# Near score tiles kept from the maxima pass and turned into the scores, in a fused two-layer kernel

## The chip, the cores and the metric

The kernel runs on one core of one Trainium2 chip, as one launch. The metric is device time in microseconds, taken as the median of several runs. A profiled execution of the same kernel gives the trace and the page that the text quotes. Engines are named as the page names them: PE is TensorE's matrix products, PEld its weight loads, DVE is VectorE, ACT is ScalarE, POOL is GpSimd and SP is the engine that issues most DMAs.

## The reference

Two layers run on x of 2 batches, 1024 tokens and 128 features. Each layer normalises x, and adds an attention and a feed-forward block that both read the normalised x.

- Layer 0: a causal attention with sigmoid in place of softmax, and a mixture of 32 experts (4 of them count for a token) with a shared expert. The kernel computes all experts for all tokens here and weighs them.
- Layer 1: a softmax attention of 16 heads of 8 features, without a causal mask, and a mixture of 16 experts with a shared one. The kernel sorts the tokens by expert, so that each token meets only its 4 experts.

The change lies in layer 1's attention, and in a few steps of the routing beside it. Cut to what matters:

```python
xn = _layernorm(x)
q, k, v = heads(xn @ Wq.T), heads(xn @ Wk.T), heads(xn @ Wv.T)      # 16 heads of 8
att_rel_pos = einsum('bhsd,pd->bhsp', q, pos_emb_k)                  # 256 positions
att_idxs = clip(ar[None, :] - ar[:, None], -128, 127) % 256
att_pos = att_rel_pos[:, :, ar[:, None], att_idxs]
att = softmax((einsum('bhqd,bhkd->bhqk', q, k) + att_pos) / sqrt(8))
y = einsum('bhqk,bhkd->bhqd', att, v)
x = x + merged(y) @ Wproj.T + experts(xn)
```

The position term depends on the distance of key and query, clipped to -128 and 127. For a query tile of 128 tokens it varies with the key only in the key tile of the same number and its two neighbours. These are the "near" tiles. In all key tiles further off it is one number per query on each side, and it can be folded into the keys.

## The kernel before, in words

**Groups and steps.** The 16 heads are handled four at a time: a slot `s` (0 to 3) holds one head in each of four row groups `r` of 32 partitions, and a product uses 32 rows of PE for each head. A group `n` is a batch, a slot and a block `q` of 512 queries (`groups`, L767). There are 16 groups, eight for each batch. Each group takes eight steps, one for each key tile `kt`, so 128 steps in all (loop at L1189). After step 67 (`EXPERTS`, L1157) the experts run in one piece, and the second batch's attention follows.

**Work of one step.** A step `t` does the following on PE, in this order:

- `scores` (L944) for step t. The scores are made turned, keys on partitions and queries along the row. First, for each near query tile, the position tile `near` is transposed into PSUM (L953, against `ident`), for row group 0, then 1, 2, 3. Then a product of keys and `qa` is added over the whole 512 columns (L963). `qa` holds the queries and, in a spare row, the negative maximum of each query. `kls` and `khs` hold the keys with the position constants of the low and the high side, and the product is split in two where the side changes. ScalarE takes the exponential of the four banks into `p` (L970).
- `values` (L974) for step t-1: `p` times `vs` into the accumulator `acc` (L982). In some steps it is split in two halves around the next item (`halved`, L1202).
- `scan` (L891) for a group ten steps ahead (`LEAD`, L768). It makes the scores unturned, for one query tile and one half of the keys (L902), and VectorE takes their maxima: far parts by a plain reduction (L927), near parts together with the `near` tile by a custom operation (L922), which writes the sum to `junk` and the maximum to `maxima`. With the second half of a query tile the two are joined and negated into `negmax` (L930). `augment` (L932) turns `negmax` and adds it to the queries to make `qa` (L937, L941).

**The near tiles.** Twice in a group `positions` (L880) runs. `by_position` (L844) multiplies queries and the position table (L853), ScalarE copies the result to `rel` (L857), and VectorE repeats its last column over 128 more (L859). A DMA takes `rel` to memory (`bounce`, L866), and another brings it back skewed by one element per row as `near` (L877).

**PSUM.** In this stage seven banks go round under the name `sm` (L1142) and one holds `acc`. `scores` and `scan` take four banks each, so a step uses one bank more than there are.

**Beside the steps.** In the first batch the second batch's gate and a counting sort (`gate1`, `sort1`, L507 and L535) run on VectorE, cut into parts by `yield`, and named one or two parts to a step (L1174). The tokens are then scattered to their experts' slots on POOL's queue (L618). In the second batch POOL gathers the experts' results, 64 tiles of 128x128 (`gather`, L626, DMA at L630), from step 68 on, some four in three steps. Each gather may start only after the last exponential of its step (`paced`, L609). Three steps later in the program (L1181) `gathered` (L636) multiplies it by its weight (L640) and adds it to `x2s` (L641), both on POOL. `operands` (L827), also on POOL, makes `kls` and `khs` (L834) and `vs` (L837) for a new slot.

**What sets the order.** The order on PE is that of the program, written out by hand (`manual_schedule`, L1187). On the other engines a planner sets each queue's order before the run, from the times at which it expects an instruction's inputs. Every engine then takes its own queue in order.

## Time and profile before

| what | us |
|---|---|
| median of 3 runs | 1305.56 |
| lowest, highest run | 1305.07, 1309.41 |
| the profiled execution's own time | 1308.08 |
| its span, first to last instruction | 1306.3 |
| exponentials, L970 (512), busy | 264.7 |
| plain maxima, L927 (472 in this stage), busy | 226.7 |
| maxima of near parts, L922 (292 in this stage), busy | 130.3 |
| product of the scores, L963 (832 with `kls`, 512 with `khs`), busy | 112.9 and 60.3 |
| transposes of near tiles, L953 (704), busy | 108.4 |
| multiply and add of gathered tiles on POOL, L640 and L641 (64 each), busy | 41.1 and 30.3 |

Busy time is the union of a group's instructions. Several matmuls run at the same time on different rows of PE, so a group's mean duration times its count is more than its busy time. In a timeline each row gives the start, the length, the engine, the line, the operation, output and inputs, and how many instructions were merged. A bracket gives the idle time of the engine ahead of it and what ended that. The mean granted clock of PE was 0.966 of full speed in this execution.

### The profile page before, as it was taken

How to read it: one execution, taken by the hardware profiler on the slowest of the kernel's cores; microseconds unless marked ns; L12 is line 12 of the kernel's file. 1: busy time of each engine (PE TensorE's matmuls, PEld its weight loads, DVE VectorE, ACT ScalarE, POOL GpSimd, SP SyncE). 2: the span in 40 equal slices, each digit the busy share in tenths (PEclk: the TensorE clock that was granted, in tenths of full speed). 3: DMA queues.
4: the chain of work that ended last, by engine and by line, in shares of the span. 5: the costliest groups of instructions: out<-in, count | busy, mean ns of one | idle time of the engine just before them, and what ended most of it. 6: DMA issues, size and time to landing. Idle time of an engine off the chain costs nothing.

```text
span 1306.3 us, 23125 instructions
## 1 busy us (share of the span) xinstructions
PE 1197.7 (92%) x8567; PEld 566.9 (43%) x8567; DVE 759.4 (58%) x2178; ACT 625.0 (48%) x1102; POOL 378.2 (29%) x464
## 2 busy tenths in 40 slices
PE   5889999989999878899799999988999999998997
PEld 2323332333333333434344354448999444443433
DVE  7783333573322358776876756764555856666653
ACT  3634444535455342454355654543444555554463
POOL 1123243323323242001002444330000445446453
PEclk9889999989999989899899999998999999998998
DMA  6682212111111261344365644659997354663511
GB/s 181 175 229 85 59 57 57 33 33 49 41 49 41 82 217 61 126 147 145 98 194 178 201 142 161 218 185 278 293 293 228 110 171 157 208 215 115 181 47 29
DMA packets 146660, 181.77 MB, mean 139 GB/s; under 512 B 16436, under 2 KB 125236, under 8 KB 146292
## 3 DMA queue, kind: packets, MB, share of 16 engines
q1 hardware_dynamic: 142292, 171.37, 42.7%
q0 software_dynamic: 4256, 8.92, 2.4%
q8 instruction: 68, 1.11, 0.4%
q14 instruction: 44, 0.36, 0.1%
HBM read 110.81 MB, written 73.77 MB: 141 GB/s over the span
## 4 chain that ended last, share of the span: by engine, by line
PE 70%; DVE 17%; DMA 5%; ACT 4%; issue 2%; POOL 1%; SPq 0%; DVEq 0%; ACTq 0%; POOLq 0%
PE sm L963 11%; PE sm L902 9%; PE acc L982 8%; PE big L340 6%; PE sm L953 5%; PE big L449 5%; PE big L341 5%; PE acc L475 5%; PE ffn L367 4%; PE sm L704 4%; DVE junk L922 3%; PE sm L853 3%; DVE maxima L927 2%; PE sm L719 2%; DMA room<-wx 1%
## 5 line engine op out<-in xcount | busy, mean ns | idle before, releaser
L970 ACT ACTIVATE p<-sm 128x512 f32<-128x512 f32 x512 | 264.7, 607 | 234.1 <-PE sm L963 233.6
L927 DVE TENSOR_REDUCE maxima<-sm 128x1 f32<-128x512 f32 (+3 forms) x472 | 226.7, 502 | 99.2 <-PE sm L902 99.2
L455 ACT ACTIVATE at<-big 128x1024 f32<-128x1024 f32 (+1 forms) x192 | 144.9, 808 | 149.7 <-PE big L449 143.7
L922 DVE CUSTOM_DVE_ANT_0 junk<-sm,near 128x384 f32<-128x384 f32 (+2 forms) x292 | 130.3, 446 | 66.3 <-PE sm L902 66.3
L982 PE MATMUL acc<-p,vs 128*32 128x512 f32 (+1 forms) x1288 | 146.4, 524 | 0.4 <-ACT yu L994 0.4
L352 DVE SCALAR_TENSOR_TENSOR t<-big,b,sg 128x512 f32<-128x512 f32 x64 | 47.9, 749 | 158.0 <-ACT sg L351 158.0
L355 POOL TENSOR_TENSOR h<-h,cb 128x512 f32<-128x512 f32 x64 | 82.8, 1294 | 195.5 <-DVE h L353 185.3
L953 PE MATMUL sm<-ident,near 128*128 128x128 f32 x704 | 108.4, 287 | 24.5 <-DVE maxima L927 11.3
L902 PE MATMUL sm<-kls,qs 32*128 32x512 f32 (+2 forms) x776 | 107.5, 580 | 6.2 <-POOL kls L834 5.0
L963 PE MATMUL sm<-qa,kls 32*128 32x512 f32 (+3 forms) x832 | 112.9, 560 | 0.0
L630 POOL DMA_INDIRECT got<-slots_y,slot_of x64 | 65.1, 1017 | 164.6 <-ACT p L970 152.5
L953 PEld LDWEIGHTS sm<-ident,near 128*128 128x128 f32 x704 | 78.0, 143 | 79.2 <-ACT p L970 35.4
L449 PE MATMUL big<-qm,xT 32*128 32x512 f32 (+3 forms) x768 | 103.8, 555 | 1.3 <-DVE xT L249 0.6
L618 POOL DMA_INDIRECT slots_x<-xn,slot_of x64 | 62.8, 981 | 95.8 <-ACT p L970 86.3
L475 PE MATMUL acc<-at,xn 128*32 128x512 f32 (+3 forms) x768 | 84.8, 514 | 5.9 <-POOL at L460 4.0
L340 PE MATMUL big<-xT,w 128*128 128x512 f32 x128 | 74.5, 665 | 14.9 <-DVE h L353 12.5
L857 ACT COPY rel<-sm 128x512 f32<-128x512 f32 x112 | 57.5, 600 | 61.6 <-PE sm L853 61.6
L640 POOL TENSOR_SCALAR got<-got,share 128x128 f32<-128x128 f32 x64 | 41.1, 642 | 110.1 <-DMA got<-slots_y,slot_of 110.0
L367 PE MATMUL ffn<-h,w 128*128 128x512 f32 x128 | 72.8, 651 | 0.0
L982 PEld LDWEIGHTS acc<-p,vs 128*32 128x32 f32 x1288 | 26.6, 109 | 105.9 <-issue 95.4
L902 PEld LDWEIGHTS sm<-kls,qs 32*128 32x128 f32 x776 | 36.9, 186 | 81.1 <-ACT p L970 21.1
L460 POOL TENSOR_SCALAR_AFFINE_SELECT at<-at 128x512 f32<-128x512 f32 x64 | 41.5, 648 | 101.6 <-ACT at L455 101.2
(285 smaller groups left out, 1659.8 us busy)
## 6 DMA issues: line engine op xcount, KB each, us to landing
bounce<-rel SPq DMA_DIRECT2D x64, 768.0 KB
near<-bounce SPq DMA_DIRECT2D x64, 768.0 KB
cb<-cw SPq DMA_DIRECT2D x128, 128.0 KB
blockw<-wx SPq DMA_DIRECT2D x53, 304.0 KB
room<-wx SPq DMA_DIRECT2D x26, 304.0 KB
slots_x<-zeros SPq DMA_DIRECT2D x19, 256.0 KB
slots_y<-by SPq DMA_DIRECT2D x19, 256.0 KB
room<-slots_x SPq DMA_DIRECT2D x17, 256.0 KB
```

What stands on the lines that cost most here:

```text
L340: nc.tensor.matmul(hh[0:m, 0, :], wa, xT, start=True, stop=True)
L367: nc.tensor.matmul(y, w2m, h[0:m], start=first, stop=last and bias_mm is None)
L449: nc.tensor.matmul(halves[r // 2][:, r % 2, off:TB], xT0[b][g, kt * P:(kt + 1) * P], masked[b, s][g, q * TB + off:(q + 1) * TB], start=Tru ...
L455: nc.scalar.activation(at[:, 2 * j:2 * j + 2, off:TB], sc[:, :, off:TB], AF.Sigmoid, scale=4.0 / math.sqrt(HD))
L475: nc.tensor.matmul(y[32 * r:32 * r + 32, off:TB], xn0[b][:, kt * P + 32 * r:kt * P + 32 * r + 32], at[:, r, off:TB], start=(kt == 0), stop ...
L902: nc.tensor.matmul(ps[r][:, (k0 - lo) * P:(k1 - lo) * P], qs[g, qt * P:(qt + 1) * P], (kh if far else kl)[g, k0 * P:k1 * P], start=True, s ...
L922: nc.vector.tensor_tensor_reduce(junk[:, 0:(k1 - k0) * P], part, near[n, i][:, r, w0:w0 + (k1 - k0) * P], 1.0, -BIG, ALU.add, ALU.max, mx[ ...
L927: nc.vector.tensor_reduce(mx[:, r, slot:slot + 1], part, AX.X, ALU.max)
L953: nc.tensor.matmul(ps[r][:, i * P:(i + 1) * P], near[n, i][:, r, w0:w0 + P], ident, is_transpose=True, start=(i == close[0]), stop=False, ...
L963: nc.tensor.matmul(ps[r][:, i0 * P:i1 * P], k[g, kt * P:(kt + 1) * P], qa[n][g, i0 * P:i1 * P], start=(m == 0 and not close), stop=(m == l ...
L970: e = nc.scalar.activation(p[:, r, :], ps[r], AF.Exp)
L982: nc.tensor.matmul(y[rows_of(r), part], vs[:, kt, rows_of(r)], probs[n, kt][:, r, part], start=(kt == 0), stop=(kt == NT - 1 and part.stop ...
```

## The change

- Near tiles: the custom operation at L922 writes its sum, position plus product, back into `near` in place of `junk`. When a query tile's maxima are complete, its negative maximum is added to the whole near tile: row groups 0 and 2 on ScalarE, 1 on POOL, 3 on VectorE. `scores` then only transposes these tiles. The product is made for the other columns alone. For every key tile these lie on one side of the near ones, so one product per row group is left. The transposes now go tile by tile with the row groups inside.
- Order of the halves: `scan` takes the step's number in its group. In a first block of queries (`q` = 0) the upper halves of all four query tiles come first, then the lower halves. In a second block each tile's lower half comes first, as before. `maxima` has six buffers in place of three.
- `rel`'s repeated column is written by POOL in place of VectorE.
- `gathered` is one operation on VectorE in place of two on POOL.
- `sort1` copies both of its products out of PSUM at once and sums in place.

```diff
--- before.py
+++ after.py
@@ -546,19 +546,17 @@
         yield
         nc.vector.tensor_add(some, some, chosen[3])
         ps = small()
-        rank, in_tile = (ps[:, i * NTT * E1:(i + 1) * NTT * E1] for i in range(2))
-        nc.tensor.matmul(rank, ahead, flat[0], start=True, stop=True)
-        nc.tensor.matmul(in_tile, ones, flat[0], start=True, stop=True)
-        rank, in_tile = (t.rearrange("p (t e) -> p t e", e=E1) for t in (rank, in_tile))
-        nc.vector.tensor_copy(some, in_tile)
-        nc.vector.memset(at[:, 0, :], 0.0)
+        for i, m in enumerate((ahead, ones)):
+            nc.tensor.matmul(ps[:, i * NTT * E1:(i + 1) * NTT * E1], m, flat[0], start=True, stop=True)
+        nc.vector.tensor_copy(flat[1], ps[:, 0:NTT * E1])
+        nc.vector.tensor_copy(flat[0], ps[:, NTT * E1:2 * NTT * E1])
         for t in range(1, NTT):
             if t % 8 == 1:
                 yield
-            nc.vector.tensor_add(at[:, t, :], at[:, t - 1, :], some[:, t - 1, :])
-        nc.vector.tensor_add(n_tok, at[:, NTT - 1, :], some[:, NTT - 1, :])
+            nc.vector.tensor_add(some[:, t, :], some[:, t, :], some[:, t - 1, :])
+        nc.vector.tensor_copy(n_tok, some[:, NTT - 1, :])
         yield
-        nc.vector.tensor_add(at, at, rank)
+        nc.vector.tensor_add(at[:, 1:, :], at[:, 1:, :], some[:, 0:NTT - 1, :])
         by_e = [P, E1, E1]
         nc.vector.tensor_tensor(some, spread(n_tok, NTT), filled.unsqueeze(1).to_broadcast(by_e), ALU.is_gt)
         nc.vector.tensor_reduce(n_blk, some, AX.X, ALU.add)
@@ -636,9 +634,7 @@
     def gathered(i):
         t, j = i // K1, i % K1
         x = x2s[t // NT][:, t % NT, :]
-        y = fetched.pop(i)
-        nc.gpsimd.tensor_scalar(y, y, share[:, t, j:j + 1], None, ALU.mult)
-        nc.gpsimd.tensor_add(x, x, y)
+        nc.vector.scalar_tensor_tensor(x, fetched.pop(i), share[:, t, j:j + 1], x, ALU.mult, ALU.add)
         if t < NT and j == K1 - 1 and t % 4 == 3:
             result(0, t // 4)
 
@@ -856,7 +852,7 @@
         for r in range(NG):
             nc.scalar.copy(rel[:, :, r, 0:2 * RAD], ps[r])
         for j in range(2):
-            nc.vector.tensor_copy(
+            nc.gpsimd.tensor_copy(
                 rel[:, j, :, 2 * RAD:NEAR],
                 rel[:, j, :, 2 * RAD - 1:2 * RAD].to_broadcast([P, NG, NEAR - 2 * RAD]),
             )
@@ -888,9 +884,11 @@
 
     maxima = {}
 
-    def scan(n, i, half):
+    def scan(n, m):
 
         b, s, q = groups[n]
+
+        i, half = (m // 2, m % 2) if q else (m % 4, 1 - m // 4)
         l1 = pools["l1"]
         qs, kl, kh, _ = head[b, s]
         qt = 4 * q + i
@@ -903,8 +901,8 @@
                     ps[r][:, (k0 - lo) * P:(k1 - lo) * P], qs[g, qt * P:(qt + 1) * P],
                     (kh if far else kl)[g, k0 * P:k1 * P], start=True, stop=True,
                 )
-        if half == 0:
-            maxima[n, i] = l1.tile([P, NG, 4], F32, tag="maxima", name="maxima", bufs=3), []
+        if (n, i) not in maxima:
+            maxima[n, i] = l1.tile([P, NG, 4], F32, tag="maxima", name="maxima", bufs=6), []
         mx, used = maxima[n, i]
         n0, n1 = max(lo, qt - 1), min(hi, qt + 2)
         if n0 >= n1:
@@ -917,17 +915,24 @@
             for r in range(NG):
                 part = ps[r][:, (k0 - lo) * P:(k1 - lo) * P]
                 if close:
-                    junk = l1.tile([P, NEAR], F32, tag="junk", name="junk")
+
                     w0 = (k0 - (qt - 1)) * P
+                    whole_ = near[n, i][:, r, w0:w0 + (k1 - k0) * P]
                     nc.vector.tensor_tensor_reduce(
-                        junk[:, 0:(k1 - k0) * P], part, near[n, i][:, r, w0:w0 + (k1 - k0) * P],
-                        1.0, -BIG, ALU.add, ALU.max, mx[:, r, slot:slot + 1],
+                        whole_, part, whole_, 1.0, -BIG, ALU.add, ALU.max, mx[:, r, slot:slot + 1],
                     )
                 else:
                     nc.vector.tensor_reduce(mx[:, r, slot:slot + 1], part, AX.X, ALU.max)
-        if half == 1:
+        if half == q:
             out_ = negmax[s, i].rearrange("p (r c) -> p r c", r=NG)[:, :, aux[s]]
             nc.vector.tensor_reduce(out_, mx[:, :, 0:len(used)], AX.X, ALU.max, negate=True)
+            w0, w1 = (max(qt - 1, 0) - (qt - 1)) * P, (min(qt + 2, NT) - (qt - 1)) * P
+            for r in range(NG):
+                t = near[n, i][:, r, w0:w1]
+                if r % 2 == 0:
+                    nc.scalar.activation(t, t, AF.Identity, bias=out_[:, r:r + 1])
+                else:
+                    (nc.gpsimd if r == 1 else nc.vector).tensor_scalar(t, t, out_[:, r:r + 1], None, ALU.add)
 
     def augment(n):
 
@@ -946,24 +951,23 @@
         b, s, q = groups[n]
         _, kl, kh, _ = head[b, s]
         ps = [small() for _ in range(NG)]
-        close = [i for i in range(4) if abs(4 * q + i - kt) <= 1]
-        for r in range(NG):
-            for i in close:
-                w0 = (kt - (4 * q + i) + 1) * P
+        c0, c1 = (min(max(kt + d - 4 * q, 0), 4) for d in (-1, 2))
+        for i in range(c0, c1):
+            w0 = (kt - (4 * q + i) + 1) * P
+            for r in range(NG):
                 nc.tensor.matmul(
                     ps[r][:, i * P:(i + 1) * P], near[n, i][:, r, w0:w0 + P], ident,
-                    is_transpose=True, start=(i == close[0]), stop=False, skip_group_check=True,
+                    is_transpose=True, start=True, stop=True,
                 )
 
-        cut = min(max(kt - 1 - 4 * q, 0), 4)
-        parts = [(0, cut, kh)] * (cut > 0) + [(cut, 4, kl)] * (cut < 4)
-        for m, (i0, i1, k) in enumerate(parts):
+        for i0, i1, k in ((0, c0, kh), (c1, 4, kl)):
             for r in range(NG):
-                g = rows_of(r)
-                nc.tensor.matmul(
-                    ps[r][:, i0 * P:i1 * P], k[g, kt * P:(kt + 1) * P], qa[n][g, i0 * P:i1 * P],
-                    start=(m == 0 and not close), stop=(m == len(parts) - 1), skip_group_check=True,
-                )
+                if i0 < i1:
+                    g = rows_of(r)
+                    nc.tensor.matmul(
+                        ps[r][:, i0 * P:i1 * P], k[g, kt * P:(kt + 1) * P], qa[n][g, i0 * P:i1 * P],
+                        start=True, stop=True,
+                    )
         p = pools["late"].tile([P, NG * TB], F32, tag="p", name="p", bufs=2)
         p = p.rearrange("p (r c) -> p r c", r=NG)
         for r in range(NG):
@@ -1100,7 +1104,7 @@
     at(N_ATT + 8, turned1, 1)
     at(N_ATT + 9, blocks1, 1)
     for m in range(LEAD):
-        at(N_ATT + 8 + m, scan, m // 8, m % 8 // 2, m % 2)
+        at(N_ATT + 8 + m, scan, m // 8, m % 8)
     at(N_ATT + 10, by_position, 1, 1)
     at(N_ATT + 13, queries, 0, 1)
     at(N_ATT + 13, operands, 0, 1)
@@ -1204,7 +1208,7 @@
                 values(n, kt, left if halved else whole)
             m = t + LEAD
             if m < N_STEPS:
-                scan(m // 8, m % 8 // 2, m % 2)
+                scan(m // 8, m % 8)
             if halved:
                 values(n, kt, right)
             for f, args in before:
```

## The prediction

> **What bounds the kernel now.** I read the engines' totals first, then the busy time by stretch, then the chain that ended last, then one step of the attention stage instruction by instruction.
>
> ```profile
> PE 1197.7 (92%) x8567; PEld 566.9 (43%) x8567; DVE 759.4 (58%) x2178; ACT 625.0 (48%) x1102; POOL 378.2 (29%) x464
> ...
> PE sm L963 11%; PE sm L902 9%; PE acc L982 8%; PE big L340 6%; PE sm L953 5%; PE big L449 5%; PE big L341 5%; PE acc L475 5%; PE ffn L367 4%; PE sm L704 4%; DVE junk L922 3%; PE sm L853 3%; DVE maxima L927 2%; PE sm L719 2%; DMA room<-wx 1%
> ```
>
> TensorE sets the end, and the second product of the scores (L963), which the change cuts, is the largest single line of the chain. The stretches say whether that holds where the change acts:
>
> ```profile
> 641.00:728.00 87.00, 84.32 (x763) 38.63 (x758) 58.76 (x192) 48.43 (x94) 13.50 (x14) 1.00 0.50 160
> ...
> 1108.00:1186.00 78.00, 70.77 (x620) 31.85 (x619) 49.72 (x156) 41.12 (x80) 38.18 (x53) 0.99 0.57 180
> ```
>
> The columns are length, then busy PE, PEld, DVE, ACT, POOL. In the first stretch PE idles 2.7 of 87 us. In the second, where gathers run, it idles 7.2 of 78. One step, with the head of the next:
>
> ```profile
> 674.39 1.27 PE L953 MATMUL sm<-ident,near 128*128 128x128 f32 x8
> 674.47 2.49 DVE L927 TENSOR_REDUCE maxima<-sm 128x1 f32<-128x512 f32 x4 [1.58 <-PE sm L902]
> 675.22 0.20 PEld L953 LDWEIGHTS sm<-ident,near 128*128 128x128 f32 x2 [0.20 <-DVE maxima L927]
> 675.59 1.14 PE L963 MATMUL sm<-qa,kls 32*128 32x512 f32 x8
> ...
> 676.66 1.07 PE L982 MATMUL acc<-p,vs 128*32 128x512 f32 x8
> 676.81 2.06 ACT L970 ACTIVATE p<-sm 128x512 f32<-128x512 f32 x4 [2.27 <-PE sm L963]
> ...
> 677.66 1.14 PE L902 MATMUL sm<-kls,qs 32*128 32x512 f32 x8
> ...
> 678.73 1.53 PE L953 MATMUL sm<-ident,near 128*128 128x128 f32 x12
> 678.81 0.42 DVE L927 TENSOR_REDUCE maxima<-sm 128x1 f32<-128x256 f32 x1 [1.65 <-PE sm L902]
> 679.15 0.42 DVE L922 CUSTOM_DVE_ANT_0 junk<-sm,near 128x256 f32<-128x256 f32 x1
> ```
>
> PE runs without a gap: transposes (0.122 us each), product (1.07 to its successor), values (1.07 less its lead, 1.00), scan (1.07). But at 675.22 the seventh transpose waits for VectorE. A step takes four banks for scores and four for the scan out of seven, so the fourth score bank is the scan's first bank, and it comes free when the scan's first row group is reduced. That decides below. Two other places where PE stands still:
>
> ```profile
> 620.73 0.73 PE L853 MATMUL sm<-posd,qs 32*128 32x256 f32 x6 [1.36 <-DVE at L561]
> ...
> 1130.82 0.60 POOL L640 TENSOR_SCALAR got<-got,share 128x128 f32<-128x128 f32 x1 [4.97 <-DMA got<-slots_y,slot_of]
> ...
> 1186.22 1.45 PE L902 MATMUL sm<-kls,qs 32*128 32x256 f32 x8 [5.03 <-POOL kls L834]
> ```
>
> The first is a bank that the sort's ranks hold until L561. The other two belong together: POOL waits for gathers to land, and the keys of the next slot (L834) stand behind them in its queue.
>
> **What the Trainium skill says.** "TensorE: Matmul & The Clock Gate", Part 3, says that products of 32 rows in different row groups run together and that matmuls keep strict order. The trace agrees: eight instructions of L963 take 1.14 us where one alone shows 0.5 to 0.6, and all of PE stands behind the one that waits. "PSUM — Partial Sum Buffer", Engine vs sequencer instructions, says that ScalarE, VectorE and GpSimd take their queues strictly in order; L834 behind the gathers agrees. "GPSIMD Engine Reference", section 4.1, advises VectorE for elementwise work, GpSimd being about half as fast with two inputs. Here L641 takes 474 ns on POOL for 128x128, and small two-input operations of that width on VectorE 0.28 us.
>
> **The change part by part.**
>
> *Second product.* A full product of four row groups costs PE 1.08 us, so one 128-wide tile of it costs 0.27. The near tiles per key tile number 2, 3, 3, 2, 1 in a first query block and 1, 2, 3, 3, 2 in a second: 11 of 32 in each of 16 groups. Removed: 16 x 11 x 0.27 = **47.5 us** of PE time. The transposes stay (704). Parts that were split at the diagonal become one part, so no weight load is added.
>
> *Order of the transposes.* Row groups were outermost: the fourth bank was first wanted after 3c transposes of c near tiles. Now tiles are outermost, and it is wanted after three: 3 x 0.122 = 0.37 us after they begin. It is free at 0.83 after a one-piece scan (675.22 less 674.39), and at about 0.96 after a two-piece one (679.57 plus 0.12 to release, less 678.73). For c=1 nothing changes (it waits already). For c=2 it was wanted at 0.73 and waited 0.10 to 0.23; the wait grows by 0.36. For c=3 it was wanted at 1.10 and did not wait; now 0.46 to 0.6, say 0.53. A group has two steps of each: 2 x 0.36 + 2 x 0.53 = 1.78, times 16 is **28.5 us given back**. Net gain of both: 19.0. What is late next is VectorE's first reduction.
>
> *Maxima subtracted.* Per query tile two 384-wide activations (ScalarE), one operation each on POOL and VectorE. ScalarE takes 0.60 for 512 and 0.38 for 256 wide, so some 0.49: 128 x 0.47 = 60 us on an engine that idles 2.3 to 2.5 us in such a step (bracket ahead of each L970). VectorE: 64 x about 0.35 = 22 us (1024 wide takes 0.79, 128 wide 0.34). POOL: L834 takes 1.19 for 1024, L640 0.6 for 128, hence 0.77 for 384: 49 us on an idle engine. The tiles are turned three steps later at the earliest, over 10 us. On ScalarE the subtraction waits for the negative maximum, 3.0 us after the scan's matmuls; exponentials of the next step may stand behind it. They are ready about 2.1 to 2.6 us after that scan. If they stand ahead, the cost is nothing; if behind, see the second rival. I take nothing.
>
> *Keys' far columns (L859) to POOL.* VectorE loses 64 x 0.45 less overlap = 24 us; POOL gains about 0.7 each (1024 wide copy: 1.04), 45 us. The bounce leaves later by about 1 us, or by 3 behind two indirect DMAs. From L859's end to the near tile's landing was 7.7 us (655.47 to 663.15). The tightest user comes three steps after, 11 to 13 us, one step earlier than before for the last tile of a first block. Hidden; without that cover 1 to 3 us in each of eight pairs of groups.
>
> *Far halves first, more maxima buffers.* Same instructions in another order: nothing.
>
> *Sort.* Both halves leave PSUM at once, so the wait on L561 goes: **1.4 us**. The chain of fifteen additions stays, and its stall of 5.26 us behind the ranks with it.
>
> *Outputs summed on VectorE.* POOL loses 64 x (0.64 + 0.47) = 71 us and 110 us of waiting; VectorE gains 64 x about 0.3 = 19 us. The stall of **5.0 us** behind L834 goes. But now VectorE waits for the gathers: a gather is released by its step's last exponential, takes POOL 1.02, and lands a further 1.72 later on average (110.0 us of idle over 64), so about 2.9 after that exponential, at worst 6 (issue at 1124.84, wait over at 1130.82). Behind the waiting sum stand the reductions of a scan, and behind them PE's banks. VectorE is done with a scan at about 681.5 and gets the next at 683.42; the gather of that step lands near 678.87 + 2.9 = 681.8. If the sum stands between two scans, an average landing is covered, and only late ones show: about ten of 64 waits pass 4.3 us, by roughly 1 us, of which I charge **6 us** in all. If it stands ahead of its own step's reductions, see the first rival.
>
> *Sum.* 1308.1 (profiled execution: 1306.3 of span, 1.8 around) - 47.5 + 28.5 - 1.4 - 5.0 + 6.0 = 1288.7. That execution lies 2.5 us (0.2%) over the median of the runs, so **1286**. Own range 1268 to 1300: up to half of the bank wait not given back, or twice the late landings. A measurement tells some 0.3% (4 us) from no change.
>
> **The rivals.**
>
> *VectorE's queue becomes the bound (slower, 0.30).* The order in an engine's queue is fixed ahead of the run. The second batch's gate shows that VectorE's work is put in as soon as its data are expected, not where the program names it: the parts that it spreads over some 14 steps ran in about four (536 to 557 us), several between the reductions of one scan. POOL's L640 likewise follows its own gather, though named three steps on. If the sums stand ahead of their own step's first reduction, a step runs from exponential to exponential as 0.2 + 2.74 (landing) + 0.25 (sum) + 0.75 (first reduction) + 0.12 + 1.15 (transposes left, product) + 0.14 + 2.06 = 7.4 us against 4.35 to 4.6. Gathers fill 48 steps; 36 of them don't split the values: 36 x 2.9 = 104 us, so **1390**, more if late subtractions on ScalarE hold exponentials too. It decides from an added wait of 0.4 us in each of the 48 steps. Against it: the POOL queue issues L837, which needs a values product of the same step, between two DMAs of that step, so a gather was allowed long, and its sum may stand behind the reductions.
>
> *Subtractions stand ahead of the next exponentials (0.15).* These then start at 3.0 + 0.9 = 3.9 us after the scan instead of 2.1 to 2.6. Where scans finish in every step (32 steps) the loop of exponential, bank, scan, reduction and subtraction takes 0.7 + 0.3 + 3.0 + 0.9 = 4.9, against some 4.3: 19 us. In the 32 others about 0.4: 13 us. 1286 + 32 less what late landings share (12): **1306**, no change.
>
> *The bank wait doesn't appear (0.12).* If reductions release it sooner, or PE makes it up elsewhere, all 47.5 count: **1257**.
>
> **How the numbers follow.** Likeliest, 0.43: 1286. Faster is that, the last rival and a little of the second: 0.57. Within 0.3%: 0.07, from the second. Slower: 0.36, the first and the rest of the second. The range runs from 1252, just under the last rival, to 1395, which holds half of the first; about 0.17 lies outside.
>
> **What would show it.** L963 should fall from 1344 instructions to 1024 at about two thirds of its time. L953 should show waits on DVE maxima of 0.4 to 0.6 us at its third or fourth instruction. In the steps with gathers, the new sums' idle time by DMA tells the first rival: under 20 us in all it is wrong, over 80 us it is right. ScalarE idle ahead of the subtractions, ended by DVE negmax, with exponentials behind, tells the second. I am wrong altogether if near tiles arrive late (PE or VectorE waiting on the near DMA) or if PE's granted clock falls with its duty.

## The result, and the profile after

The changed kernel takes **1503.8 us** (median of 4 runs, 1499.65 to 1511.91) against 1306.61 before on the same chip (1305.07 to 1309.41): ratio 1.151, 95% interval 1.146 to 1.157. The forecast was 1286, with a range up to 1395. The direction, the size and the range were all wrong.

First the page of the changed kernel: engine totals, then PE's granted clock in 40 slices, then some groups (busy us, mean ns, then idle time ahead and what ended it). Lines have moved: exponentials are L974, transposes L958, products L967, scan L900, reductions L925 and L921, subtractions L933 and L935, sums L637.

```profile
PE 1286.6 (86%) x8247; PEld 597.6 (40%) x8247; DVE 774.9 (52%) x2242; ACT 687.9 (46%) x1230; POOL 429.5 (29%) x464
...
PEclk9899999999998988979889989999988767778788
...
L958 PE MATMUL sm<-ident,near 128*128 128x128 f32 x704 | 129.7, 319 | 79.1 <-DVE maxima L925 57.4
L935 POOL TENSOR_SCALAR near<-near,negmax 128x384 f32<-128x384 f32 (+1 forms) x64 | 85.7, 1339 | 389.4 <-DVE negmax L928 332.8
...
L933 ACT ACTIVATE near<-near,negmax 128x384 f32<-128x384 f32 (+1 forms) x128 | 68.2, 582 | 162.9 <-DVE negmax L928 162.8
...
L637 DVE SCALAR_TENSOR_TENSOR x<-got,share,x 128x128 f32<-128x128 f32 x64 | 23.1, 360 | 132.5 <-DMA got<-slots_y,slot_of 132.2
```

PE has 320 instructions fewer, as intended, and is busy for 89 us more. The clock went with it: its mean fell from 0.966 to 0.899, so the same work took PE longer. The sums wait 132 us for gathers on VectorE (the forecast's test for its first rival was 80), ScalarE's subtractions wait 163 us for the negative maximum (its test for the second), and the transposes wait 57 us for reductions. ScalarE and POOL work 63 and 51 us more, but spread over the whole span; what stands out is how long the engines wait for each other. The sort did what was said: no line waits for a sort copy for more than 0.8 us.

The two stretches of the forecast, now over the same steps (20 to 38 and 87 to 102; columns as before, the last but two is the granted clock):

```profile
656.67:758.89 102.22, 92.96 (x680) 39.23 (x680) 57.78 (x185) 54.70 (x109) 30.95 (x32) 0.88 0.42 133
1219.81:1339.42 119.61, 94.38 (x592) 38.93 (x586) 54.98 (x183) 46.03 (x90) 38.09 (x39) 0.76 0.37 117
```

These steps took 83.8 and 71.0 us before, both at a clock of 1.00. So both batches lost, the second, with its gathers, much more.

One step of the first batch, from the changed kernel's timeline:

```profile
788.07 1.09 ACT L974 ACTIVATE p<-sm 128x512 f32<-128x512 f32 x2 [4.61 <-PE sm L967]
788.81 0.17 DVE L928 TENSOR_REDUCE negmax<-maxima 128x4 f32<-128x12 f32 x1
...
789.04 0.90 ACT L933 ACTIVATE near<-near,negmax 128x256 f32<-128x256 f32 x2
...
789.84 1.08 ACT L974 ACTIVATE p<-sm 128x512 f32<-128x512 f32 x2
...
790.49 0.33 PE L958 MATMUL sm<-ident,near 128*128 128x128 f32 x1 [0.16 <-ACT p L974]
...
791.52 0.55 DVE L921 CUSTOM_DVE_ANT_0 near<-sm,near 128x384 f32<-128x384 f32 x1
...
792.00 0.88 DVE L925 TENSOR_REDUCE maxima<-sm 128x1 f32<-128x128 f32 x4
792.35 1.33 PE L958 MATMUL sm<-ident,near 128*128 128x128 f32 x5 [1.04 <-DVE maxima L925]
...
793.12 1.12 ACT L933 ACTIVATE near<-near,negmax 128x384 f32<-128x384 f32 x2 [2.20 <-DVE negmax L928]
...
794.92 2.06 ACT L974 ACTIVATE p<-sm 128x512 f32<-128x512 f32 x4 [0.68 <-PE sm L967]
```

Three things stand here. Two of four exponentials stand behind two subtractions (789.04), and PE's transposes wait for them bank by bank. VectorE takes all four near pieces (L921, up to 792.00) before the first L925, so a bank comes free only at 792.3, and the fourth transpose waits for it. And at 793.12 ScalarE has stood 2.20 us for the next negative maximum.

A stretch with gathers, same kernel:

```profile
1204.78 0.35 DVE L637 SCALAR_TENSOR_TENSOR x<-got,share,x 128x128 f32<-128x128 f32 x1 [3.15 <-DMA got<-slots_y,slot_of]
...
1205.05 0.68 DVE L925 TENSOR_REDUCE maxima<-sm 128x1 f32<-128x512 f32 x1
...
1208.88 0.35 DVE L637 SCALAR_TENSOR_TENSOR x<-got,share,x 128x128 f32<-128x128 f32 x1 [1.16 <-DMA got<-slots_y,slot_of]
1209.15 0.42 DVE L925 TENSOR_REDUCE maxima<-sm 128x1 f32<-128x256 f32 x1
...
1210.89 0.91 ACT L933 ACTIVATE near<-near,negmax 128x256 f32<-128x256 f32 x2 [4.85 <-DVE negmax L928]
...
1211.70 1.55 ACT L974 ACTIVATE p<-sm 128x512 f32<-128x512 f32 x3
```

The sum at 1208.88 stands in the middle of one scan's reductions. It waits for its gather, the rest of the scan waits for it, the negative maximum for the scan, the subtraction for that, and an exponential for the subtraction. Both rivals act in one chain.

The start of each step's first exponential, read from the traces, gives the time by stretch. The four columns of times run from the start of step 1 to that of step 66, on to that of step 67 (the experts lie in between), of step 115 and of step 127. The last column, clock loss, is (1 - mean clock) x span. It is an upper bound for what PE lost, since it also counts half rate while PE had nothing to do:

| kernel | 1 to 66 | experts | 67 to 115 | 115 to 127 | clock loss |
|---|---|---|---|---|---|
| before | 350.1 | 132.6 | 239.8 | 38.9 | 43.8 |
| changed | 401.0 | 137.7 | 377.1 | 41.2 | 151.4 |
| e1_sums_back | 399.7 | 131.5 | 301.0 | 41.6 | 97.4 |
| e3_sums_alone | 350.2 | 134.4 | 351.0 | 40.5 | 92.5 |
| e5_paced | 383.6 | 133.9 | 278.1 | 38.0 | 86.1 |
| e9_three | 334.1 | 133.5 | 236.3 | 37.7 | 38.6 |
| e12_product_alone | 336.0 | 135.9 | 272.5 | 36.4 | 63.4 |
| e13_adds_off_pool | 331.9 | 136.7 | 235.7 | 36.4 | 43.7 |
| e14_before_no_junk | 377.9 | 130.3 | 253.5 | 40.1 | 47.3 |
| e17_unpaced | 385.8 | 137.6 | 368.3 | 43.2 | 139.2 |
| e18_subs_early | 373.6 | 135.8 | 278.4 | 43.6 | 76.1 |
| e19_sums_early | 339.4 | 133.5 | 348.4 | 38.2 | 103.3 |

### The profile page after: what moved, and what is told of

It reads as the page before. It is cut to its first block, busy times and chain, and to the rows that moved or that the text cites. A ratio compares the mean times of both kernels' runs of the same rounds, so it can differ in the third digit from the quotient of the medians.

```text
span 1501.3 us, 22819 instructions
## 1 busy us (share of the span) xinstructions
PE 1286.6 (86%) x8247; PEld 597.6 (40%) x8247; DVE 774.9 (52%) x2242; ACT 687.9 (46%) x1230; POOL 429.5 (29%) x464
## 5 line engine op out<-in xcount | busy, mean ns | idle before, releaser
L974 ACT ACTIVATE p<-sm 128x512 f32<-128x512 f32 x512 | 266.2, 602 | 206.1 <-PE sm L967 205.8
L925 DVE TENSOR_REDUCE maxima<-sm 128x1 f32<-128x512 f32 (+3 forms) x472 | 222.2, 501 | 148.9 <-PE sm L900 148.7
L958 PE MATMUL sm<-ident,near 128*128 128x128 f32 x704 | 129.7, 319 | 79.1 <-DVE maxima L925 57.4
L935 POOL TENSOR_SCALAR near<-near,negmax 128x384 f32<-128x384 f32 (+1 forms) x64 | 85.7, 1339 | 389.4 <-DVE negmax L928 332.8
L986 PE MATMUL acc<-p,vs 128*32 128x512 f32 (+1 forms) x1288 | 167.2, 594 | 0.6 <-ACT yu L998 0.6
L921 DVE CUSTOM_DVE_ANT_0 near<-sm,near 128x384 f32<-128x384 f32 (+2 forms) x292 | 124.5, 445 | 68.0 <-PE sm L900 52.9
L900 PE MATMUL sm<-kls,qs 32*128 32x512 f32 (+2 forms) x776 | 144.0, 621 | 15.0 <-ACT p L974 8.0
L958 PEld LDWEIGHTS sm<-ident,near 128*128 128x128 f32 x704 | 92.1, 160 | 135.0 <-DVE maxima L925 64.5
L933 ACT ACTIVATE near<-near,negmax 128x384 f32<-128x384 f32 (+1 forms) x128 | 68.2, 582 | 162.9 <-DVE negmax L928 162.8
L849 PE MATMUL sm<-posd,qs 32*128 32x256 f32 x448 | 67.7, 477 | 36.9 <-DVE maxima L925 36.7
L900 PEld LDWEIGHTS sm<-kls,qs 32*128 32x128 f32 x776 | 47.0, 203 | 128.0 <-ACT p L974 45.5
L637 DVE SCALAR_TENSOR_TENSOR x<-got,share,x 128x128 f32<-128x128 f32 x64 | 23.1, 360 | 132.5 <-DMA got<-slots_y,slot_of 132.2
L967 PE MATMUL sm<-qa,khs 32*128 32x512 f32 (+3 forms) x512 | 76.3, 598 | 4.5 <-DVE maxima L925 2.9
```

The source lines that it names most:

```text
L900: nc.tensor.matmul(ps[r][:, (k0 - lo) * P:(k1 - lo) * P], qs[g, qt * P:(qt + 1) * P], (kh if far else kl)[g, k0 * P:k1 * P], start=True, s ...
L921: nc.vector.tensor_tensor_reduce(whole_, part, whole_, 1.0, -BIG, ALU.add, ALU.max, mx[:, r, slot:slot + 1],)
L925: nc.vector.tensor_reduce(mx[:, r, slot:slot + 1], part, AX.X, ALU.max)
L935: (nc.gpsimd if r == 1 else nc.vector).tensor_scalar(t, t, out_[:, r:r + 1], None, ALU.add)
L958: nc.tensor.matmul(ps[r][:, i * P:(i + 1) * P], near[n, i][:, r, w0:w0 + P], ident, is_transpose=True, start=True, stop=True,)
L967: nc.tensor.matmul(ps[r][:, i0 * P:i1 * P], k[g, kt * P:(kt + 1) * P], qa[n][g, i0 * P:i1 * P], start=True, stop=True,)
```

## The experiments

Every run below has its ratio to before on the same chip in the same session, with a 95% interval. Before moved by some 0.3% between sessions (1301.8 to 1306.1), so kernels of different sessions are compared by ratio; 1% is 13 us.

### First round: which queue

**e1_sums_back** puts the old `gathered` back in the changed kernel:

```diff
-        nc.vector.scalar_tensor_tensor(x, fetched.pop(i), share[:, t, j:j + 1], x, ALU.mult, ALU.add)
+        y = fetched.pop(i)
+        nc.gpsimd.tensor_scalar(y, y, share[:, t, j:j + 1], None, ALU.mult)
+        nc.gpsimd.tensor_add(x, x, y)
```

> The changed kernel with one part undone: the outputs are summed on POOL again, by two operations each. Theory 1 (queue order: on VectorE the sums wait for gathers ahead of a scan's reductions, on ScalarE the subtractions wait for the negative maxima ahead of exponentials): the 48 steps with gathers lose about 100 of the 138 us that they gained, since the first batch, which has no gathers, lost 51 us in 66 steps, or 37 per 48. So about 1405, and VectorE's wait for gathers is gone. Rival A (PE's granted clock fell for a reason of its own and drags everything): the time stays above 1480. Rival B (subtractions on ScalarE hold the steps in the second batch too, and the sums only fill a wait that is there anyway): above 1470, with the idle time ahead of the subtractions grown.

Measured: 1424.69 us, ratio 1.092 (1.090 to 1.095). Steps 67 to 115 became 76 us shorter, the first batch 1. So the sums cost much of it, as theory 1 has it, but 20 us less came back than expected. Two lines of its waits (us in total, times, the longest) say where the rest stays:

```profile
ACT near L935 <- DVE negmax L930: 122.3, 45, 7.2
...
DVE near L923 <- DMA near<-bounce: 55.0, 7, 16.3
```

Near tiles now come up to 16.3 us late: POOL's far columns of the keys (moved there by the change) stand behind its sums, which wait for gathers.

**e2_no_scalar** gives ScalarE's subtractions away:

```diff
-                if r % 2 == 0:
-                    nc.scalar.activation(t, t, AF.Identity, bias=out_[:, r:r + 1])
-                else:
-                    (nc.gpsimd if r == 1 else nc.vector).tensor_scalar(t, t, out_[:, r:r + 1], None, ALU.add)
+                if True:
+                    (nc.gpsimd if r % 2 else nc.vector).tensor_scalar(t, t, out_[:, r:r + 1], None, ALU.add)
```

> The changed kernel with ScalarE's two subtractions per query tile given to VectorE and POOL (two each there); the sums stay on VectorE. Theory 1: exponentials no longer stand behind a wait for the negative maximum; the first batch (steps 1 to 66) loses 30 to 50 of its 51 us, the second some 20 to 40 of its 138: 1415 to 1455. VectorE pays 64 more operations of 0.41 us. Rival C (the fourth score bank, wanted early by the new order of the transposes, holds the first batch): the first batch loses at most 15 us, 1485 or more. Rival A: as C, and the clock stays near 0.90.

Measured: 1481.45 us, ratio 1.134 (1.132 to 1.136), the first batch 389.6: 11 us less. Theory 1 had said 30 to 50. So something other than ScalarE's queue held the first batch too, and rival C was nearer. It is no clean removal, since VectorE and POOL each take 64 more subtractions here.

**e3_sums_alone** makes one part of the change alone, the new `gathered`, in the kernel before.

> The kernel before with one part of the change alone: the outputs summed on VectorE by one operation each. Theory 1: the sums stand between and ahead of the reductions of their own step, so steps with gathers take about 6.5 to 7.4 us in place of 4.3 to 4.9: 1390 to 1410, with 80 us or more of VectorE's idle time ended by gathers. Rival (the forecast's own step 6: the sum stands between two scans): 1303 to 1315. Rival B: 1330 at most, since no subtraction holds ScalarE here.

Measured: 1411.9 us, ratio 1.081 (1.078 to 1.083), 105 us over before. The first batch did not move (350.2), the steps with gathers grew by 111 us. The forecast's first rival, priced at 104, is shown by one edit, and the forecast's own step for the sums (the expectations call it step 6) is refuted.

**e5_paced** moves no work; it sets two orders (the edit, shortened):

```diff
 def gathered(i):
-        nc.vector.scalar_tensor_tensor(x, fetched.pop(i), share[:, t, j:j + 1], x, ALU.mult, ALU.add)
+        d = nc.vector.scalar_tensor_tensor(x, fetched.pop(i), share[:, t, j:j + 1], x, ALU.mult, ALU.add)
+        paced(d)
 def scan(n, m):
-                    nc.scalar.activation(t, t, AF.Identity, bias=out_[:, r:r + 1])
+                    owed.append((t, out_[:, r:r + 1]))
 def scores(n, kt):
         last_exp["name"] = e.ins.name
+        for t, m in owed:
+            paced(nc.scalar.activation(t, t, AF.Identity, bias=m))
+        owed.clear()
```

(The scans ahead of step 0 subtract at once.)

> The changed kernel with nothing moved to another engine, only two orders changed: each sum is put behind the last exponential of the step in which the program names it (three steps after its gather), and ScalarE's two subtractions behind the exponentials of the next step. Theory 1: both waits go, and what is left is the forecast's sum without its term for late landings: 1280 to 1300. Rival C (transposes and the fourth score bank): 1330 or more, with waits of L953's successor for VectorE's maxima of over 60 us in all. Rival A: 1400 or more at a clock near 0.90.

Measured: 1376.75 us, ratio 1.053 (1.051 to 1.056). The two orders are worth 9.8%, 128 us, but 70 us remained, 33 of them in the first batch. Theory 1 was half of it.

### Second round: what holds the paced kernel

Its timeline showed near tiles late (SPq is SP's queue, and its row is the time of issuing DMAs, not of their landing) and, as in the step shown above, four near pieces ahead of the first bank.

```profile
756.00 3.29 SPq L874 DMA_DIRECT2D near<-bounce  x2
...
764.49 0.29 DVE L922 CUSTOM_DVE_ANT_0 near<-sm,near 128x128 f32<-128x128 f32 x1 [4.32 <-DMA near<-bounce]
```

**e6_paced_rows**: in `scores` of e5_paced, `for r` outside `for i` again.

> The paced kernel (e5_paced, 1377 us) with the transposes put back into the order of before, row groups outermost. Theory 1 (the forecast's second step: the fourth score bank is wanted too early): some 28 us come back, 1345 to 1355. Theory 2 (the reductions release that bank so late, after all four near pieces of a scan, that the order of the transposes matters little): 5 to 15 us, 1362 to 1372.

Measured: 1357.33 us, ratio 1.043 (1.038 to 1.048). That is 14 us by ratio and 19 by medians: between the two theories.

**e7_scan_order**: in `scan` of e5_paced, the halves' order of before.

```diff
-        i, half = (m // 2, m % 2) if q else (m % 4, 1 - m // 4)
+        i, half = m // 2, m % 2
...
-        if half == q:
+        if half == 1:
```

> The paced kernel (e5_paced) with the scan's order of before: both halves of one query tile after each other, in first blocks too. Theory 3 (near tiles late: with far halves first the fourth tile of a first block is wanted three steps after its products in place of six, and VectorE waits 4.3 us for it once in each pair of groups): the step that is 10.3 us long falls to about 6, eight times 4.5 us, 36 in all: 1335 to 1345. Rival: the wait moves to the next late thing, a gain under 10 us: 1367 or more.

Measured: 1327.94 us, ratio 1.020 (1.015 to 1.024): 44 us by ratio. The step that took 10.4 us takes 7.1, and the next ones are shorter too. Theory 3 holds. VectorE's 27.6 us of waits for near tiles in e5_paced are gone. The fourth tile of a first block is wanted three steps after its product, and VectorE gets it at 764.49, 12.2 us after the end of its far columns (752.3 on POOL).

**e8_row_by_row**: in `scan` of e5_paced, `for r` outside the pieces, so that VectorE finishes a row group at a time.

> The paced kernel (e5_paced) with the loops of a scan's reductions swapped, so that VectorE takes both pieces of a row group after each other, as it did before the change; now it takes all four near pieces and then all four others wherever the near piece comes first, and the first bank comes free at about 2.2 us in place of 0.8. Theory 2: five scans in each pair of groups, about 1 us each, and more where by-position products follow: 30 to 45 us, 1332 to 1347. Rival (the banks are not what these steps wait for): under 10 us, 1367 or more.

Measured: 1351.72 us, ratio 1.036 (1.031 to 1.042): 22 us by ratio, some less than expected. Theory 2 holds in kind.

**e9_three**: all three.

> The paced kernel with all three of these together: transposes row group by row group, the scan's order of before, reductions row group by row group. What remains of the change is the missing second product, the subtractions (late), the sums on VectorE (late), far columns on POOL and the sort. If theories 1 to 3 name all that was lost: the forecast's sum without its second step and late landings, 1308 less 47.5, 1.4 and 5.0, so 1255 to 1275. If PE's clock or another wait holds (rival A): 1300 or more.

Measured: 1292.9 us, ratio 0.994 (0.991 to 0.998). The three are worth 77 us together, and the kernel is 0.6% faster than before, less than expected. The clock is back at 0.970, without any edit to PE's rate: rival A falls.

**e14_before_no_junk** asks why the order on VectorE changed. In the kernel before, the sums of the near pieces go to the bank they came from:

```diff
-                        junk[:, 0:(k1 - k0) * P], part, near[n, i][:, r, w0:w0 + (k1 - k0) * P],
+                        part, part, near[n, i][:, r, w0:w0 + (k1 - k0) * P],
```

> The kernel before with one edit: the sums of the near pieces, which nobody reads there, are written over the bank of scores that they come from, and not into the one buffer junk. Theory 2 (that one buffer, taken in turn, is what kept VectorE's two pieces of a row group together; without it the program's order shows, four near pieces and then four others, and the first bank comes free about 1.4 us later in five scans of each pair of groups): 15 to 35 us slower, 1317 to 1337. Rival (the order comes from another part of the change, or the later bank is covered): within 5 us of 1302.

Measured: 1348.17 us, ratio 1.032 (1.030 to 1.035). In its trace all four near pieces stand ahead of the others in 15 scans, where the changed kernel has 16 such scans, and in others a part of them. In the kernel before the two kinds take turns in every one. So the single buffer `junk` had kept the pieces of a row group together, and to drop it is enough to lose that. The 42 us are an upper end for the order: VectorE is also busy 19 us longer (778.3 against 759.4), since the closing part of each near operation takes 0.14 us with a bank as its target, where it took 0.08.

### Third round: the single terms

**e10_two_steps** is e9_three with the subtractions held back through a second list, one more step.

> e9_three with ScalarE's subtractions one step later still (behind the exponentials of the second step after their scan). In e9_three one step in 16 still takes 10.8 us against 7.2 before: two subtractions (1.12 us) stand ahead of the copy of a finished group's values, VectorE waits 0.97 us for that copy with three reductions behind it. If that is the cause: 1.1 to 1.5 us in each of eight steps, 9 to 12 us, so about 1282. Rival (the 1.84 us that VectorE then takes for an operation that took 0.75 before, beside a copy on POOL, sets it): under 4 us, 1289 or more.

Measured: 1289.99 us, ratio 0.988 (0.985 to 0.990). The long step (median 10.8 in the first batch) falls to 7.3, and the one ahead of it rises from 4.0 to 5.0, so the cause is right and a part of the gain moves. The whole is 8 us by ratio and 3 by medians, with a longer profiled span (1293.5 against 1288.5, the experts' stage 3 us of that): its size is not settled.

**e11_columns_back** is e9_three with `nc.vector.tensor_copy` for the far columns.

> e9_three with the far columns of the keys back on VectorE. The forecast's fourth step took the move at nothing for either engine: 1288 to 1298. Rival (VectorE's reductions are what the steps with by-position products wait for, so 64 copies of 0.4 us there count in part): 1300 to 1312. Rival (near tiles leave earlier from VectorE, and some were late): 1280 to 1286.

Measured: 1292.82 us, ratio 0.990 (0.987 to 0.993). The intervals overlap with e9_three's: on either engine the columns cost nothing that can be told here.

**e12_product_alone** is e11_columns_back with the sums on POOL (the diff of e1_sums_back).

> The missing second product alone, with the subtractions and the sort: outputs summed on POOL and far columns on VectorE, as before; transposes row group by row group, the scan's order of before, reductions row group by row group, ScalarE's subtractions late. If the forecast's first step holds (47.5 us of PE time, and the sort's 1.4): 1250 to 1262. If the subtractions and VectorE's reductions give part of it back, as in e9_three: 1275 to 1295. Difference to e9_three: what the paced sums and the moved columns are worth, which the forecast put at 5 us in their favour.

Measured: 1332.9 us, ratio 1.022 (1.019 to 1.025), outside both cases. The first batch is as in e9_three; the steps with gathers are 36 us longer. A line of its waits tells why:

```profile
PE sm L962 <- POOL near L939: 45.2, 8, 13.0
```

Transposes wait up to 13 us for POOL's subtraction, which stands behind sums that wait for gathers.

**e13_adds_off_pool** gives that subtraction to VectorE: `nc.vector.tensor_scalar` for row groups 1 and 3.

> e12_product_alone with POOL's one subtraction per query tile given to VectorE. In e12 TensorE's transposes wait 45 us for POOL's subtraction, in eight waits of up to 13 us, all in stretches with gathers, where POOL's queue also holds the sums that wait for them. If that collision is all that e12 lost to e9_three: 1333 less 45, plus a little for 64 operations of 0.42 us more on VectorE: 1280 to 1293. Rival (sums on POOL hold something else, the next slot's keys or the gathers' own issue): 1305 or more.

Measured: **1286.54 us**, ratio 0.983 (0.981 to 0.986). The collision was most of what e12 lost, but the rival is there too. POOL still waits 108 us for gathers, and its two copies of the next slot's keys stand behind the sums that wait for them:

```profile
PE sm L902 <- POOL khs L832: 7.6, 1, 7.6
...
PE sm L902 <- POOL kls L832: 5.6, 1, 5.6
```

Both waits fall in one step, which takes 23.1 us, where it took 14.4 before and 6.4 in e9_three. With the next run it is the fastest version.

**e16_off_pool_two_steps**, both of the last ideas:

> e13_adds_off_pool with ScalarE's subtractions one step later, the difference between e9_three and e10_two_steps, which was under 0.7%: within 6 us of e13_adds_off_pool, that is 1276 to 1293 if that one comes out as expected. It is the candidate for the fastest version.

Measured: 1286.6 us, ratio 0.984 (0.982 to 0.987): the same as e13_adds_off_pool.

**e15_product_again** is e10_two_steps with a product by `zeros` after each near tile's transposes:

```diff
+        for i in range(c0, c1):
+            for r in range(NG):
+                g = rows_of(r)
+                nc.tensor.matmul(
+                    ps[r][:, i * P:(i + 1) * P], kl[g, kt * P:(kt + 1) * P], zeros[g, 0:P],
+                    start=False, stop=True, skip_group_check=True,
+                )
```

> e10_two_steps with the second product of the near tiles put back as work alone: after its transposes each near tile takes a product with a tile of zeros in all four row groups, which adds nothing to the scores. It tells what the missing product is worth. Forecast's first step: 16 groups of 11 tiles by 0.27 us, 47.5 us: 1332 to 1342. Rival (half of it lay beside waits for banks): 1308 to 1320. Rival (with each wait TensorE's clock falls too, so that less slack costs double): no change of that, since more work makes no wait.

The near tiles' scores are not kept whole in this kernel, which is read for its time alone. Measured: 1324.92 us, ratio 1.015 (1.012 to 1.017), 35 us over e10_two_steps, between the two cases. The product is worth some 35 of the forecast's 47.5. This is an estimate: the stand-in is 704 products of 128 columns, 1408 instructions more, where the change had taken away 320. PE is busy only 26 us longer (1195.9 against 1169.9), and its clock is higher (0.976).

**e17_unpaced** is e9_three without both paced orders; **e18_subs_early** lacks only that of the subtractions, **e19_sums_early** only that of the sums.

> e9_three without its two paced orders: the changed kernel with only the transposes, the scan's order and the reductions put right. Theory 1 (sums waiting in VectorE's queue cost by themselves what e3_sums_alone showed, 105 us, and ScalarE's early subtractions some 15 to 25): 1400 to 1425. Rival (the waits in the queues hurt only because banks and near tiles were late already, and vanish with them): 1300 to 1330.

> e9_three with only ScalarE's subtractions put back where the planner places them; the sums stay paced. It sizes the forecast's second rival by itself. The rival's own price was 32 us: 1320 to 1330. From e17_unpaced, whose first batch (no gathers, so no sums) took 52 us more than e9_three's, the 48 steps with gathers should lose some 38 more: 1370 to 1395.

> e9_three with only the sums on VectorE put back where the planner places them; ScalarE's subtractions stay late. It sizes the forecast's first rival by itself. The rival's own price was 104 us: 1390 to 1405. If the two waits add up to what e17_unpaced lost (184 us) and the subtractions take 90 of it: 1380 to 1395. If they share steps, so that either alone makes most of it: 1420 or more.

Measured, in this order: 1476.7 us, ratio 1.128 (1.124 to 1.133), outside both of its cases; 1381.8, 1.058 (1.055 to 1.062), as reckoned from e17_unpaced; 1404.7, 1.076 (1.074 to 1.078), at the top of the rival's price. Over e9_three's 0.994 that is 175, 84 and 107 us. So each wait is a cause by itself, and they add up but for 16 us. The first rival's price was met, the second's 32 too low by more than half. The first batch of e18, without a sum in it, lost 40 us to early subtractions. e2_no_scalar had shown only 11, probably because there late near tiles and banks held the same steps; that was not tried apart.

## Why the prediction was wrong, step by step

- *Second product, 47.5 us.* The mechanism was right: 1024 of the 1344 instructions are left. It was mis-sized: some 35 us (e15_product_again).
- *Order of the transposes, 28.5 us back.* Right in kind: 14 to 19 us (e6_paced_rows, where the bank came late anyway). But the step took the bank's release (0.83 to 0.96 us) from the old order of VectorE's reductions. Writing to `near` in place of `junk` freed the planner to put all four near pieces first; that term, 22 us (e8_row_by_row), was missing. I listed what the operation writes, not what the one buffer had been ordering.
- *Maxima subtracted, "I take nothing".* This step failed first. I set ScalarE's idle time against the work, 60 us (68 in the trace); the cost is the wait, 84 us (e18_subs_early). The rival priced it as one step's loop. In the step shown above two of four exponentials stand behind the subtractions, so PE's transposes wait as well.
- *POOL's subtraction.* Forecast at 0.77 us, 49 in all; it takes 1.34, 85.7 in all. No wait of PE for it shows while the sums stand on VectorE (e9_three), but behind the sums on POOL it cost PE 45 us of waits (e12_product_alone).
- *Far columns to POOL.* Nothing, as forecast, in e9_three (e11_columns_back). In e1_sums_back, where they stand behind the sums on POOL, near tiles came up to 16.3 us late.
- *Far halves first, "nothing".* This failed too; it is worth 44 us (e7_scan_order). I named the tightest user, three steps or 11 to 13 us on, and called it hidden by a landing 7.7 us after the far columns. That was misread. The time 663.15 is the end of this row of the kernel before, which is the issue of the pair's second DMA:

```profile
659.52 3.63 SPq L877 DMA_DIRECT2D near<-bounce  x2
```

In that trace the transfer's last semaphore update comes at 667.40, 11.9 us after the far columns. In e5_paced the same row ends at 759.29, and the tile is there at 764.49, 12.2 us after them. So there was no slack that could hide a user three steps on, whichever engine copies the columns.
- *Sort, 1.4 us.* Its wait is 0.8 us or less.
- *Sums on VectorE, +1 net.* The step that failed most. "If the sum stands between two scans" was the choice; the sums stand inside scans. They cost 105 us (e3_sums_alone) and 107 (e19_sums_early). That the rival's 104 comes so close is in part luck: it counts nothing for the clock, which is a large part of the loss (below). The gain of 5.0 us is real: with the sums on VectorE, PE no longer waits for POOL's keys (e9_three). By the gaps ahead of L640 six of the 64 waits passed 4.3 us, not ten. The evidence of the other kind was in my own text: VectorE's gate parts ran as soon as expected, between the reductions of one scan. I let one DMA on POOL's queue outweigh it.
- *What would make it wrong.* Both were named: late near tiles, and PE's clock falling with its duty. The first had a price only for the move of the far columns, 1 to 3 us in each of eight pairs; the clock had none.

**The clock adds to the waits.** "TensorE: Matmul & The Clock Gate", Part 1, says that PE has a full and a half rate, that at least one idle window of about 3.4 us brings the half rate and that at least one busy window of that length ends it. The traces agree on the two rates and not on the idle time needed. In e9_three PE stood idle for 1.28 us from 775.7 on, and the stretches show what followed (the third number from the end is the granted clock):

```profile
776.00:778.00 2.00, 1.05 (x3) 0.58 (x4) 2.00 (x4) 0.76 (x2) 1.86 (x3) 0.97 0.92 333
778.00:780.00 2.00, 2.00 (x18) 1.72 (x17) 0.89 (x3) 0.00 (x0) 1.38 (x2) 0.50 0.40 146
780.00:782.00 2.00, 2.00 (x15) 1.50 (x12) 2.00 (x10) 0.01 (x1) 0.00 (x0) 0.50 0.63 188
782.00:784.00 2.00, 2.00 (x8) 1.35 (x8) 1.24 (x5) 2.00 (x4) 0.97 (x1) 0.50 0.00 0
784.00:786.00 2.00, 2.00 (x21) 1.41 (x22) 0.00 (x0) 0.42 (x2) 1.61 (x3) 0.82 0.01 5
```

From 778 on PE is busy throughout, and at half rate for some 6.8 us: by this estimate about 3.4 us more are lost than the wait itself. The next idle time of 1.28 us, at 855.7, was followed by the half rate in the same way. In e3_sums_alone the profiled span grew by 111 us and the clock loss by 49; in e19_sums_early by 116 (over e9_three) and 65. So the clock makes up at most 44 and 56% of what these waits cost. It is not so for every loss: e14_before_no_junk is 42 us slower with 3.5 us more of clock loss. That the clock follows the waits and not the other way is argued from the table, where the loss falls as waits are removed; no run set the clock alone.

**What stays open.** The product is worth some 35 us, and the best version gains 22. Of the 13 us between, 8 can be read in e13_adds_off_pool: PE's two waits for POOL's keys, 13.2 us together, against one of 5.0 before. No run put the keys ahead of the sums there. The rest is not traced; VectorE's 128 subtractions are a candidate. One step of 7 to 9 us in sixteen is not, since it takes as long in the kernel before (medians of 7.0 and 8.5 us in the two batches). The paced sums on VectorE are no free choice either: in e9_three they wait 54 us there for the exponential behind which they are set.

## What to carry to other kernels

An operation moved to an engine with idle time brings its waits into that engine's queue: ask what it waits for, when that is ready, and who stands behind, before counting its own length. A scratch buffer with one copy may be what holds a good order; when it goes, write the order down (swap the loops, or pace the late step behind a named instruction). Where TensorE is near its limit, a new wait may cost up to about twice its length (e19_sums_early), so price the clock as a range of its own. Follow each transfer to its landing, and not to the end of its issue.

## What the runs showed of the hardware

- In e9_three PE fell to half rate after 1.28 us of idle time, for some 6.8 us. What the limit is, no run shows.
- An addition of one number per partition, 128x384, took 1339 ns on POOL and 414 on VectorE (means in which one in four is 128x256), 3.2 times, where 0.77 us was expected from a 1024 wide one of 1.19 us.
- An operation of 0.75 us on VectorE took 1.84 us once in e9_three (774.45) while POOL ran a copy of 1.05; the kernel before has one of 2.33. Whether POOL causes it was not tried.
